# Layer 1 of a ternary feed-forward kernel by Strassen's seven products, on one Trainium2 core

## The chip, the core and the metric

The kernel runs on one NeuronCore of a Trainium2 chip. The core has a matrix engine (TensorE, PE in the profile; its weight loads are shown apart as PEld), a vector engine (DVE), a scalar engine (ACT), a general engine (GpSimd, POOL) and a queue that only starts transfers (SP). Each works through its own instructions in order, and semaphores tell one engine that another has finished. PE reads SBUF, the on-chip memory of 128 partitions, and writes PSUM, a small accumulation memory of eight banks of 2 KB per partition; ACT and DVE read both, POOL only SBUF. The metric is the time of one execution on the device in microseconds, lower is better; the median of the runs is given, and the profile is of one execution.

## The reference

```python
# x (128, 64, 512), conditions (128,), weights (200, 64, 64),
# W1 (2048, 512), b1 (2048,), W2 (512, 2048), b2 (512,)
w = weights[conditions]
c = jnp.einsum('bct,bcd->bdt', x, w)               # mixing by a condition

def ternary_linear(x, W, b, threshold=0.05):
    Wq = ternarize(W, threshold)                   # alpha * sign(W) * (|W| > 0.05 max|W|)
    return jnp.einsum('bsd,hd->bsh', x, Wq) + b

h = gelu(ternary_linear(c, W1, b1))                # (128, 64, 2048)
y = ternary_linear(h, W2, b2)                      # (128, 64, 512)
scale = jnp.max(jnp.abs(y)) / 7 + 1e-8             # over all of y
return x + jnp.clip(jnp.round(y / scale), -7, 7) * scale
```

The ternary weights without alpha are -1, 0 and 1, so they are exact in any type; alpha is applied once per layer behind the matmuls.

## The kernel before

**Tiling.** The 128 sequences of 64 tokens are 8192 tokens. A block is 512 of them (4 pairs of sequences); there are NB = 16 blocks. The 2048 hidden features are NH = 16 chunks of 128. The ternary weights lie in SBUF for good, as 1-byte numbers: `w1t` (per chunk 4 x 128 inputs by 128 features) and `w2t` (per chunk 128 features by 512 outputs).

**Precision.** Matmuls run on a 32-bit type that keeps fewer bits (float32r, shown as fp32r or f32). So each activation is split into a high part, rounded by ACT, and a low part, the rest, by DVE (`split`, lines 197 to 200), and each matmul is done for both. The weights are widened to the same type by POOL just before use (`widen1`, `widen2`, lines 415 to 430), into small rotating buffers `w1f` and `w2f`.

**One step** (n, hc), lines 713 to 748, is one chunk of one block. POOL widens the weights of the next step's layer 1 and of the previous step's layer 2. PE does `layer1`: 8 matmuls (4 input pieces, 2 parts) of 512 tokens into one bank, `ph`. ACT takes the bank with Gelu, bias and alpha into `hf` and rounds it to the high part, and DVE subtracts (`bend`, lines 446 to 449). Then PE does `layer2` for the chunk of two steps before (LAG = 2): 8 matmuls of 512 outputs into four banks, `py0` to `py3`, which add up over the 16 chunks of a block. When the last chunk is in, DVE writes y out of the four banks (`result`) and takes its maxima (`largest`).

**Conditioning** of the next block is spread over the steps of this one: SP loads x (`load_x`), POOL gathers the condition matrices (`fetch`) and places them on a block diagonal (`place`), and in four steps (hc 8 to 11) PE mixes one pair each (`mix`, 4 matmuls in source, 8 on the engine since they are done in full precision, of 128 columns, into a bank `pc`), from which ACT and DVE make the two parts of `x` (`condition`, lines 213 to 216).

**The order** on each engine is the order of the source: the wrapper `InOrder` (lines 43 to 51) passes every instruction through and keeps it. That is why the profile puts almost all of them on line 51, and why they are told apart by the names of their tiles.

**Ends.** Before this loop the weights are loaded and made ternary while block 0 runs in another order (lines 107 to 700). After it, the scale over all y is made, x is loaded again, and the result is written (lines 750 to 815).

**Buffers.** The pool `big` has 22 buffers of 8 KB per partition, `half` has 6 of 4 KB (w1f, w2f, hf and three for the parts of h), `ps_h` two banks, `ps_c` two, `ps_y` four. A buffer given out again makes its first writer wait for the last reader of the one before.

Of the kernel before, what the change touches and what calls it, by code (L numbers as in the profile page):

```python
# [22 lines left out]
F32 = mybir.dt.float32  # L26
# [28 lines left out]
def tile_cond_ternary_ffn(  # L55
# [26 lines left out]
    GH = NH // NG  # L82
    WCH = GH * T
    LAG = 2

    const = ctx.enter_context(tc.tile_pool(name="const", bufs=1))
    big = ctx.enter_context(tc.tile_pool(name="big", bufs=22))
    gather = ctx.enter_context(tc.tile_pool(name="gather", bufs=PAIRS))
    half = ctx.enter_context(tc.tile_pool(name="half", bufs=6))
    ps_c = ctx.enter_context(tc.tile_pool(name="ps_c", bufs=2, space=PSUM))  # L90
    ps_h = ctx.enter_context(tc.tile_pool(name="ps_h", bufs=2, space=PSUM))
    ps_y = ctx.enter_context(tc.tile_pool(name="ps_y", bufs=1, space=PSUM))
# [4 lines left out]
    def pair_of_pairs(h):  # L97
        return slice(h * PAIRS // 2, (h + 1) * PAIRS // 2)

    def load_x(n):  # L100
        xt = big.tile([P, PAIRS, T], F32, tag="big", name=f"xt_{n}")
        for h in range(2):
            js = pair_of_pairs(h)
            sp.dma_start(out=xt[:, js, :], in_=x_blk[n][:, js, :])
        return xt

# [85 lines left out]
    def parts(n):  # L194
        return [big.tile([P, NT, BLK], F32R, tag="big", name=f"x{k}_{n}") for k in range(2)]

    def split(src, hi, lo, engine=dve):

        act.copy(hi, src)
        engine.tensor_tensor(lo, src, hi, ALU.subtract)  # L200

    def mix(xt, j, pc):

        for c in range(NT):
            pe.matmul(
                out=pc[:, c, :],
                lhsT=xt[:, j, c * P : (c + 1) * P],
                rhs=diag[:, j, :],
                start=True,
                stop=True,  # L210
            )
# [179 lines left out]
    pb = ps_c.tile([P, NH], F32, tag="pc", name="pb")  # L391
    pe.transpose(pb, b1n, ident_f[:NH, :NH])
    b1t = const.tile([P, NH], F32)
    w1f0 = big.tile([P, 4, NT, P], F32R, tag="big", name="w1f0")
    turned(act, w1f0[:, 0], 0)
    hi0(2)
    hi0(3)
    turned(act)
# [5 lines left out]


    hidden = {}
    wide1 = {(0, 0): w1f0[:, 0]}
    wide2 = {}
    ypsum = {}
    ys = []  # L410
# [3 lines left out]

    def widen1(n, hc):

        w = w1f0[:, hc % 4] if n == 0 else w1f[:, hc % 2]
        pool.tensor_copy(w, w1t[:, hc])
        wide1[n, hc] = w

    def widen2(n, hc):
        if n == 0 and hc < NH - LAG:
            w = w2f0[0][:, hc % 4]
        elif n == NB - 1 and hc == NH - 1:

            w = w1f[:, 0].rearrange("p c h -> p (c h)")
        else:
            w = w2f[:, hc % 2]
        pool.tensor_copy(w, w2t[:, hc])
        wide2[n, hc] = w  # L430

# [14 lines left out]

    def bend(n, hc, ph, two, hf, engine=dve):
        act.activation(hf, ph, AF.Gelu, bias=b1t[:, hc : hc + 1], scale=alpha[1])
        split(hf, *two, engine)
        hidden[n, hc] = two  # L450

    def layer2(n, hc, js=range(PAIRS)):
        two = hidden[n, hc]
        w = wide2[n, hc]
        if hc == 0:
            ypsum[n] = [
                ps_y.tile([P, T], F32, tag=f"py{j}", name=f"py{j}_{n}") for j in range(PAIRS)
            ]
        for j in js:
            for k in range(2):  # L460
                pe.matmul(
                    out=ypsum[n][j],
                    lhsT=two[k][:, j * P : (j + 1) * P],
                    rhs=w,
                    start=(hc == 0 and k == 0),
                    stop=(hc == NH - 1 and k == 1),
                )
# [13 lines left out]

    waiting = {}
    pairs0 = {}
    ring = big.tile([P, 4, BLK], F32, tag="big", name="ring")

    def early(hc):

# [8 lines left out]
    def early_bend(hc):  # L496
        if hc % 2 == 0:
            pairs0[hc // 2] = big.tile([P, 2, 2, BLK], F32R, tag="big", name=f"h_{hc}")
        h = pairs0[hc // 2]
        bend(  # L500
            0,
            hc,
            waiting.pop(hc),
            [h[:, hc % 2, k, :] for k in range(2)],
            ring[:, hc % 4, :],
            pool if hc % 2 == 0 and hc < 10 else dve,
        )

# [111 lines left out]
    early_bend(0)  # L620
    x_next = load_x(1)
    two_next = parts(1)
    find = thresholds("w2", top_2, above.bitcast(F32)[:, :P])
    made = {}
    w2f0 = []
    puts = {}

    def put(key):
# [13 lines left out]
    def behind(hc):  # L642
        if hc in (6, 8, 10, 11):
            put({8: 7}.get(hc, hc))
        if hc in (5, 6, 8):
            largest2({5: 1, 6: 2, 8: 3}[hc])
        if hc == 7:
            signed1(3)
        if hc == 10:
            next(find)  # L650
            delta.extend(next(find))
            made[0] = signed2(0)
            next(made[0])
        if hc == 11:
            next(made[0])
        if hc == 14:
            put("2a")
        if hc == 15:
            w2f0.append(big.tile([P, 4, T], F32R, tag="big", name="w2f0"))
            widen2(0, 0)  # L660

    for hc in range(5, NH):
# [30 lines left out]
        if 8 <= hc < 8 + NG:  # L693
            sum2(hc - 8)
    cond[1] = two_next
    w1f = half.tile([P, 2, NT, P], F32R, tag="half", name="w1f")
    w2f = half.tile([P, 2, T], F32R, tag="half", name="w2f")
    hf = half.tile([P, 2, BLK], F32, tag="half", name="hf")
    widen1(1, 0)
    widen2(0, NH - LAG)  # L700


    steps = [(n, hc) for n in range(NB) for hc in range(NH)]
# [6 lines left out]
            j = hc // (NH // PAIRS)  # L710
            sp.dma_start(out=dying[t][:, j, :], in_=x_blk[3 + t][:, j, :])

    for s in range(NH, len(steps)):
        n, hc = steps[s]
        if s + 1 < len(steps):
            widen1(*steps[s + 1])
            lend(0, *steps[s + 1])
        widen2(*steps[s + 1 - LAG])
        lend(1, *steps[s + 1 - LAG])
        if n + 1 < NB:  # L720
            if hc == 0:
                x_next = load_x(n + 1)
                two_next = parts(n + 1)
                fetched = []
            if 2 <= hc < 2 + PAIRS:
                fetched.append(fetch(n + 1, hc - 2))
            if 7 <= hc < 7 + PAIRS:
                place(hc - 7, fetched[hc - 7])
        if n == NB - 1 and hc < 3:
            again.append(load_x(hc))  # L730
        ph = ps_h.tile([P, BLK], F32, tag="ph", name=f"ph_{n}_{hc}")
        layer1(n, hc, ph)
        two = half.tile([P, 2, BLK], F32R, tag="half", name=f"h_{n}_{hc}")
        bend(n, hc, ph, [two[:, k, :] for k in range(2)], hf[:, hc % 2, :])
        if n + 1 < NB and 8 <= hc < 8 + PAIRS:
            condition(n + 1, hc - 8, x_next, two_next)
            cond[n + 1] = two_next
        if hc == LAG:
            for j in range(PAIRS):
                largest(n - 1, j)  # L740
        if s == len(steps) - 1:
            break
        if s == NH + 1:
            alpha_2()
        layer2(*steps[s - LAG])
        if steps[s - LAG][1] == NH - 1:
            for j in range(PAIRS):
                result(n - 1, j)

    n = NB - 1  # L750
    widen2(n, NH - 1)
    lend(1, n, NH - 1)
    again += [t for t in dying]
    for _ in range(2):
        again.append(load_x(len(again)))
    dve.tensor_reduce(
# [22 lines left out]
    dve.reciprocal(inverse, scale)  # L779


    halves = []
    for i in range(6):
        m, h = len(again) + i // 2, i % 2
        xt = half.tile([P, PAIRS // 2, T], F32, tag="half", name=f"xt_{m}_{h}")
        sp.dma_start(out=xt, in_=x_blk[m][:, pair_of_pairs(h), :])
        halves.append(xt)
    xs = [[xt[:, pair_of_pairs(h), :] for h in range(2)] for xt in again]
    xs += [halves[i : i + 2] for i in (0, 2, 4)]
    quant = flat(diag).bitcast(I8).rearrange("p (k t) -> p k t", k=PAIRS)  # L790
    AHEAD = len(xs)
    for n in range(NB):

        while len(xs) < min(AHEAD + 3 * n // 2, NB):
            xt = load_x(len(xs))
            xs.append([xt[:, pair_of_pairs(h), :] for h in range(2)])
        for h in range(2):


            q = quant[:, h * PAIRS // 2 : (h + 1) * PAIRS // 2, :]  # L800
            if n < NB - 1:
                y = res = ys[n][:, pair_of_pairs(h), :]
                act.activation(flat(q), flat(y), AF.Identity, scale=inverse)
                dve.scalar_tensor_tensor(
                    flat(y), flat(q), scale, flat(xs[n][h]), ALU.mult, ALU.add
                )
            else:
                res = xs[n][h]
                for k in range(PAIRS // 2):
                    y = ypsum[n][h * PAIRS // 2 + k]  # L810
                    act.activation(q[:, k, :], y, AF.Identity, scale=inverse)
                    dve.scalar_tensor_tensor(
                        res[:, k, :], q[:, k, :], scale, res[:, k, :], ALU.mult, ALU.add
                    )
            pool.dma_start(out=out_blk[n][:, pair_of_pairs(h), :], in_=res)
# [34 lines left out]
```

## Time and profile before

| | us |
|---|---|
| median of 3 runs | 1102.17 (1100.96 to 1102.38) |
| the profiled execution | 1102.12 |
| its span, from the first to the last instruction | 1100.4 |
| one block in the middle (238.1 to 300.0, from one block's first layer 2 to the next's) | 61.9 |
| PE busy | 1023.9 |
| ACT, POOL, DVE busy | 471.6, 466.7, 399.2 |

How to read the lines of the profile: engine, operation, the tile that is written, an arrow, the tiles that are read, then partitions x elements and types of output and input. In a group "x2040 | 514.3, 394 | 0.0" is the number of instructions, their busy time in us, the mean duration of one in ns, and the engine's idle time just before them with the operation that ended it. In the timeline a line has its start, its length and how many neighbouring instructions of one kind are merged in it; "[2.93 <-ACT h L51]" is idle time before it and what ended it. Matmuls overlap in the array, so the duration of one is longer than the time from one to the next. The chain of waits goes back from the last instruction through whatever released each; its shares say which engine set the end.

### The profile page before, as it was taken

Reading aid. Unit: us, or ns where it says so; the run is one execution under the profiler, and the core shown is the slowest. Engines: PE = TensorE matmul, PEld = TensorE weight load, DVE = VectorE, ACT = ScalarE, POOL = GpSimd, SP = SyncE. Lnnn points to the kernel's source line nnn. Section 1 sums busy time; section 2 is a strip of 40 time slices with the busy share of each in tenths; the row PEclk is TensorE's granted clock in tenths of the full one; section 3 lists DMA queues with packets and bytes.
Section 4 is the critical chain, followed back from the end, with each engine's and each line's share of the span. In section 5 each row is a group of like instructions: output and inputs, shape, how many; then the busy total and the mean of one; then the engine's idle time right before and its main releaser. Section 6 shows DMA issues by size and latency. Waiting matters only on the chain.

```text
span 1100.4 us, 13296 instructions
## 1 busy us (share of the span) xinstructions
PE 1023.9 (93%) x4830; PEld 841.4 (76%) x4832; DVE 399.2 (36%) x549; ACT 471.6 (43%) x650; POOL 466.7 (42%) x754
## 2 busy tenths in 40 slices
PE   8989999999999999999999999999999999999500
PEld 4678788888888888888888888888888888888400
DVE  6875423232322323232322423232322423232592
ACT  6965333434344433434344343434344343434491
POOL 5644535343443535343443535343443535333242
PEclk9999999999999999999999999999999999999855
DMA  9214001000101001000001001000001001111699
GB/s 327 78 39 153 5 1 44 1 5 4 38 5 38 6 1 44 1 4 6 36 4 39 6 2 43 1 4 7 35 5 39 6 3 42 39 58 39 254 416 380
DMA packets 28752, 62.01 MB, mean 56 GB/s; under 512 B 2816, under 2 KB 2960, under 8 KB 28688
## 3 DMA queue, kind: packets, MB, share of 16 engines
q1 hardware_dynamic: 22032, 42.28, 11.2%
q0 software_dynamic: 6656, 18.88, 4.4%
q8 instruction: 39, 0.64, 0.3%
q14 instruction: 25, 0.20, 0.1%
HBM read 44.38 MB, written 16.78 MB: 56 GB/s over the span
## 4 chain that ended last, share of the span: by engine, by line
PE 89%; DVE 4%; DMA 4%; ACT 2%; issue 1%; POOL 0%; POOLq 0%; DVEq 0%; ACTq 0%
PE py L51 42%; PE ph L51 40%; PE pc L51 5%; DMA out<-y 4%; PE idle L51 2%; DVE tern L51 1%; DVE top L51 1%; DVE y L51 0%; PE pt L51 0%; DVE h L51 0%; ACT diag L51 0%; ACT h L51 0%; DVE ymax L51 0%; DVE py L51 0%; ACT ring L51 0%
## 5 line engine op out<-in xcount | busy, mean ns | idle before, releaser
L51 PE MATMUL py<-w2f,h 128*128 128x512 f32 x2040 | 514.3, 394 | 0.0
L51 PE MATMUL ph<-x,w1f 128*128 128x512 f32 (+1 forms) x2056 | 507.5, 389 | 1.0 <-POOL w1f L51 0.7
L51 PEld LDWEIGHTS ph<-x,w1f 128*128 128x128 f32 x2056 | 384.5, 188 | 81.5 <-POOL w1f L51 1.0
L51 PEld LDWEIGHTS py<-w2f,h 128*128 128x128 f32 x2040 | 377.6, 189 | 80.5 <-DVE y L51 5.5
L51 ACT ACTIVATE hf<-ph,b1t,alpha_w 128x512 f32<-128x512 f32 x240 | 187.2, 780 | 554.1 <-PE ph L51 554.1
L51 DVE TENSOR_TENSOR h<-hf,h 128x512 fp32r<-128x512 f32 x240 | 166.2, 692 | 650.6 <-ACT h L51 650.6
L51 POOL CAST w2f<-w2t 128x512 fp32r<-128x512 fp8e4 x255 | 178.6, 701 | 360.1 <-PE py L51 336.3
L51 POOL CAST w1f<-w1t 128x512 fp32r<-128x512 fp8e4 x255 | 163.6, 643 | 192.8 <-PE ph L51 180.2
L51 ACT CAST h<-hf 128x512 fp32r<-128x512 f32 x240 | 148.8, 620 | 7.6
L51 PEld LDWEIGHTS pc<-diag,xt 128*128 128x128 f32 x512 | 66.6, 192 | 4.6
L51 POOL DMA_INDIRECT wg<-in_L_cond_weights,rows x64 | 63.6, 994 | 13.7 <-issue 6.6
L51 PE MATMUL pc<-diag,xt 128*128 128x128 f32 x512 | 67.6, 276 | 0.0
L51 DVE TENSOR_TENSOR x<-pc,x 128x512 fp32r<-128x512 f32 x64 | 43.6, 684 | 10.2 <-ACT x L51 10.2
L51 DVE SCALAR_TENSOR_TENSOR y<-py,alpha_w,b2b 128x512 f32<-128x512 f32 x60 | 40.8, 742 | 0.1
L51 ACT ACTIVATE diag<-y,inverse 128x1024 int8<-128x1024 f32 x30 | 34.3, 1148 | 12.1 <-DVE inverse L51 8.8
L51 ACT CAST x<-pc 128x512 fp32r<-128x512 f32 x64 | 37.1, 582 | 5.5 <-PE pc L51 5.5
L51 POOL DMA_DIRECT2D out<-y x30 | 21.8, 728 | 40.0 <-DVE y L51 25.9
L51 DVE TENSOR_REDUCE ymax<-y 128x1 f32<-128x512 f32 x60 | 36.9, 676 | 0.0
L51 DVE SCALAR_TENSOR_TENSOR y<-diag,scale,xt 128x1024 f32<-128x1024 int8 x26 | 32.4, 1282 | 6.4 <-DMA xt<-in_x 4.9
L51 POOL COPY diag<-wg 64x64 f32<-64x64 f32 x128 | 29.6, 231 | 8.3 <-DMA wg<-in_L_cond_weights,rows 4.5
L51 PE MATMUL idle<-junk,ones_b 128*128 128x512 bf16 x63 | 16.7, 433 | 3.4 <-POOL junk L51 3.3
L51 PEld LDWEIGHTS <-ones_b 128*128 128x128 bf16 x80 | 8.3, 106 | 14.9 <-issue 6.3
(91 smaller groups left out, 205.1 us busy)
## 6 DMA issues: line engine op xcount, KB each, us to landing
xt<-in_x SPq DMA_DIRECT2D x60, 512.0 KB, 4.7
out<-y POOLq DMA_DIRECT2D x30, 512.0 KB, 12.8
nat<-in_L_ffn_W SPq DMA_DIRECT2D x7, 1024.0 KB, 13.2
nat<-in_L_ffn_W SPq DMA_DIRECT2D x2, 512.0 KB, 12.8
wg<-in_L_cond_weights,rows POOLq DMA_INDIRECT x64, 2.4
w1t<-in_x SPq DMA_DIRECT2D x4, 256.0 KB, 2.7
w2t<-in_x SPq DMA_DIRECT2D x4, 256.0 KB, 2.6
out<-xt POOLq DMA_DIRECT2D x2, 512.0 KB, 9.5
```

Of the source, the lines that this page charges most:

```text
L51: return lambda *args, **kw: self._tc.keep_in_program_order(make(*args, **kw))
```

## The change

For blocks 2 to 11 (`SEVEN`), two chunks of layer 1 are computed together. The product of a 2 x 2 scheme of halves (halves of the 512 inputs; chunk 2k and chunk 2k+1 of features; the first and the second 64 tokens of each pair of sequences, `b11`, `b12`, `b21`, `b22`) is formed from seven products of halves in the order of Winograd's variant, in place of eight.

- Weights: four combinations `w1s` of w1t (`combine`), made by DVE once, in block 1. `widen7` widens, per pair of chunks, the seven left factors in four groups. The buffers `w1f` and `w2f` now have four slots each for the whole run and are used in twos outside `SEVEN`.
- Activations: `condition7` makes, besides the halves b11, b21 and b22, four combinations `t` in full precision (DVE) and their two parts.
- `seven`: 28 matmuls of 256 tokens into three banks: `x` and `y` (the two of ps_h, which change places from pair to pair) and `z` (one of ps_c, with p4 and p5 in its halves). Some products add onto a bank that ACT has copied out before. ACT copies x, z and x into `ring` (ha and hb, the sums of the two chunks); DVE adds y, p5 and the last x; then Gelu runs in place. The layer 2 of the two chunks before is done in eight pieces (`second`, 2 matmuls each) between the products. The second chunk's Gelu is issued at the start of the next pair (`finish`), and the low parts of h by `low`.
- Loads, gathers, placing, the conditioning of the next block and the maxima of y are issued at fixed places of the pairs (`behind`); the conditioning in pairs 3 to 6.
- Buffers: big 20, half 10. Block 15's x and some reloads of x go to pairs of half buffers. Blocks 0, 1 and 12 to 15 keep the old step, now called `eight`.

```diff
-    big = ctx.enter_context(tc.tile_pool(name="big", bufs=22))
+    big = ctx.enter_context(tc.tile_pool(name="big", bufs=20))
-    half = ctx.enter_context(tc.tile_pool(name="half", bufs=6))
+    half = ctx.enter_context(tc.tile_pool(name="half", bufs=10))
...
     def bend(n, hc, ph, two, hf, engine=dve):
         act.activation(hf, ph, AF.Gelu, bias=b1t[:, hc : hc + 1], scale=alpha[1])
-        split(hf, *two, engine)
+        if engine is None:
+            act.copy(two[0], hf)
+            open_low[n, hc] = lambda: dve.tensor_tensor(two[1], hf, two[0], ALU.subtract)
+        else:
+            split(hf, *two, engine)
...
+    def combine():
+        w1s = big.tile([P, NH // 2, 4, 2 * P], F8, tag="big", name="w1s")
+        extra["w1s"] = w1s
+        s1, s2, s4, s3 = (w1s[:, :, i, :] for i in range(4))
+        for out, in0, in1, op in (
+            (s1, a21, a22, ALU.add),
+            (s2, s1, a11, ALU.subtract),
+            (s4, a12, s2, ALU.subtract),
+            (s3, a11, a21, ALU.subtract),
+        ):
+            dve.tensor_tensor(out, in0, in1, op, saturate=False)
+            yield
+
+    def groups(k):
+        w1s = extra["w1s"]
+        return (
+            ((0, 0, T, w1t_f[:, 2 * k]),),
+            ((1, 0, T // 2, w1s[:, k, 0]), (1, T // 2, T, w1t_f[:, 2 * k + 1, T // 2 :])),
+            ((2, 0, T, flat(w1s[:, k, 1:3])),),
+            ((3, 0, T // 2, w1s[:, k, 3]),),
+        )
+
+    def widen7(k, g):
+        for i, lo, hi, src in groups(k)[g]:
+            pool.tensor_copy(flat(w1f[i])[:, lo:hi], src)
...
+    def condition7(n, j, xt, two):
+        xb, xts, xl = two
+        cols = slice(j * C, (j + 1) * C)
+        pc = ps_c.tile([P, NT, P], F32, tag="pc", name=f"pc_{n}_{j}")
+        mix(xt, j, pc)
+        act.copy(xb[:, 0, :, cols], pc[:, :, :C])
+        act.copy(xl[:, 0, :, cols], pc[:, 2:, C:])
+        t, b12 = extra["t"], extra["b12"]
+        act.copy(b12, pc[:, :2, C:])
+        dve.tensor_tensor(t[:, 0], b12, pc[:, :2, :C], ALU.subtract)
+        dve.tensor_tensor(t[:, 2], pc[:, 2:, C:], b12, ALU.subtract)
+        dve.tensor_tensor(t[:, 1], pc[:, 2:, C:], t[:, 0], ALU.subtract)
+        dve.tensor_tensor(t[:, 3], pc[:, 2:, :C], t[:, 1], ALU.subtract)
+        dve.tensor_tensor(xb[:, 1, :, cols], pc[:, :, :C], xb[:, 0, :, cols], ALU.subtract)
+        dve.tensor_tensor(xl[:, 1, :, cols], pc[:, 2:, C:], xl[:, 0, :, cols], ALU.subtract)
+        t8 = t.rearrange("p a c d -> p (a c) d")
+        hi, lo = (x.rearrange("p a c d -> p (a c) d")[:, :, cols] for x in xts)
+        act.copy(hi, t8)
+        dve.tensor_tensor(lo, t8, hi, ALU.subtract)
+
+    def product(out, w, b, first):
+        for c in range(2):
+            for k in range(2):
+                pe.matmul(out=out, lhsT=w[:, c, :], rhs=b[k][:, c, :],
+                    start=(first and c == 0 and k == 0), stop=(c == 1 and k == 1),
+                    skip_group_check=True)
+
+    def seven(n, k, behind, second):
...
+        behind(0)
+        product(x, w1f[0][:, :2], b11, True)
+        act.copy(ha_2[:, 0], turned(x))
+        product(y, w1f[0][:, 2:], b21, True)
+        behind(1)
+        dve.tensor_tensor(ha_2[:, 0], turned(y), ha_2[:, 0], ALU.add)
+        product(p5, w1f[1][:, :2], t1, True)
+        product(p4, w1f[1][:, 2:], t4, False)
+        behind(2)
+        act.copy(hb_2, z.rearrange("p (h j d) -> p h j d", h=2, j=PAIRS))
+        second(0)
+        product(x, w1f[2][:, :2], t2, False)
+        act.copy(ha_2[:, 1], turned(x))
+        second(1)
+        second(2)
+        product(p5, w1f[2][:, 2:], b22, False)
+        dve.tensor_tensor(ha_2[:, 1], turned(p5), ha_2[:, 1], ALU.add)
+        second(3)
+        bend7(0, ha)
+        behind(3)
+        second(4)
+        product(x, w1f[3][:, :2], t3, False)
+        dve.tensor_tensor(
+            hb_2, turned(x).unsqueeze(1).to_broadcast([P, 2, PAIRS, C]), hb_2, ALU.add
+        )
+        low(n, 2 * k)
+        behind(4)
+        for i in range(5, 8):
+            second(i)
+        return lambda: bend7(1, hb)
...
+        def behind(i):
+            if i == 0:
+                finish()
+                widen2(*before[1])
+                if k == 0:
+                    x_next.append(load_x(n + 1))
+                    two_next.append(parts7(n + 1) if n + 1 in SEVEN else parts(n + 1))
+            if i == 1:
+                low(*before[1])
+                if leaves:
+                    widen1(n + 1, 0)
+                else:
+                    widen7(ahead, 0)
+            if i == 2:
+                if not leaves:
+                    widen7(ahead, 1)
+                if k in (0, 1):
+                    for j in (2 * k, 2 * k + 1):
+                        fetched.append(fetch(n + 1, j))
+                if k in (2, 3):
+                    for j in (2 * k - 4, 2 * k - 3):
+                        place(j, fetched[j - PAIRS])
+            if i == 3:
+                widen2(*steps[s])
+                if not leaves:
+                    widen7(ahead, 2)
+            if i == 4:
+                if not leaves:
+                    widen7(ahead, 3)
+                if 3 <= k < 3 + PAIRS:
+                    make = condition7 if n + 1 in SEVEN else condition
+                    make(n + 1, k - 3, x_next[-1], two_next[-1])
+                    cond[n + 1] = two_next[-1]
+                if k in (1, 2):
+                    for j in (2 * k - 2, 2 * k - 1):
+                        largest(n - 1, j)
```

## The prediction

> **What bounds the kernel now.** First the page: busy times, granted clock and the chain that ended last.
>
> ```profile
> PE 1023.9 (93%) x4830; PEld 841.4 (76%) x4832; DVE 399.2 (36%) x549; ACT 471.6 (43%) x650; POOL 466.7 (42%) x754
> ...
> PEclk9999999999999999999999999999999999999855
> ...
> PE py L51 42%; PE ph L51 40%; PE pc L51 5%; DMA out<-y 4%; PE idle L51 2%; DVE tern L51 1%; DVE top L51 1%; DVE y L51 0%; PE pt L51 0%; DVE h L51 0%; ACT diag L51 0%; ACT h L51 0%; DVE ymax L51 0%; DVE py L51 0%; ACT ring L51 0%
> ```
>
> PE is the bound: layer 2 (py), layer 1 (ph) and the mixing (pc) are 87% of the chain, at full clock until the output stage. ACT, DVE and POOL are under half busy, so work moved to them is free only as long as PE never waits for its result. Next, PE in order of time: what one matmul costs in a run.
>
> ```profile
> 25.32 1.12 PE L51 MATMUL ph<-x,w1f 128*128 128x256 f32 x8
> ```
> ```profile
> 500.60 1.98 PE L51 MATMUL ph<-x,w1f 128*128 128x512 f32 x8
> ```
> ```profile
> 506.04 1.05 PE L51 MATMUL pc<-diag,xt 128*128 128x128 f32 x8
> ```
>
> A merged line ends with the last matmul's own duration. 256 columns (chunk 0 of block 0 is computed in two halves, so the form is in this trace): mean 0.28, hence (1.12-0.28)/7 = 0.120 us from start to start. 512 columns: (1.98-0.39)/7 = 0.2266. 128 columns: 0.111. A half-width matmul costs 53% of a full one, not 50%. Third, the chain in order of time shows the one regular wait of PE, at each block's start: a layer-2 chunk of 1.99 instead of 1.81, of which the end of a merged line and the wait for DVE's y leave about 0.17 lost per block.
>
> ```profile
> 482.45 1.81 PE ph L51 x8
> 484.26 1.99 PE py L51 x8
> ```
>
> Fourth, the groups by shape, for the small operations that the change adds (mean ns is the number before the last bar):
>
> ```profile
> L51 ACT ACTIVATE hf<-ph,b1t,alpha_w 128x512 f32<-128x512 f32 x240 | 187.2, 780 | 554.1 <-PE ph L51 554.1
> L51 ACT CAST h<-hf 128x512 fp32r<-128x512 f32 x240 | 148.8, 620 | 7.6
> L51 ACT CAST x<-pc 128x512 fp32r<-128x512 f32 x64 | 37.1, 582 | 5.5 <-PE pc L51 5.5
> ...
> L51 ACT CAST w2t<-pt 128x1024 fp8e4<-128x1024 bf16 x8 | 8.1, 1010 | 13.5 <-PE pt L51 13.5
> ...
> L51 ACT ACTIVATION_READ_ACCUMULATOR tern<-tern 128x1 f32 x4 | 0.8, 195 | 0.0
> ```
> ```profile
> L51 DVE TENSOR_TENSOR h<-hf,h 128x512 fp32r<-128x512 f32 x240 | 166.2, 692 | 650.6 <-ACT h L51 650.6
> L51 DVE TENSOR_TENSOR x<-pc,x 128x512 fp32r<-128x512 f32 x64 | 43.6, 684 | 10.2 <-ACT x L51 10.2
> ...
> L51 DVE TENSOR_TENSOR first<-first 128x128 f32<-128x128 f32 x1 | 0.3, 293 | 0.0
> ```
>
> Last, single hand-overs in order of time:
>
> ```profile
> 90.24 1.05 PE L51 MATMUL pc<-diag,xt 128*128 128x128 f32 x8
> ...
> 91.33 0.59 ACT L51 CAST x<-pc 128x512 fp32r<-128x512 f32 x1 [1.77 <-PE pc L51]
> ```
> ```profile
> 507.05 0.62 ACT L51 CAST h<-hf 128x512 fp32r<-128x512 f32 x1
> 507.57 0.58 ACT L51 CAST x<-pc 128x512 fp32r<-128x512 f32 x1
> 507.70 0.69 DVE L51 TENSOR_TENSOR h<-hf,h 128x512 fp32r<-128x512 f32 x1 [2.93 <-ACT h L51]
> ```
> ```profile
> 1027.27 0.62 ACT L51 CAST h<-hf 128x512 fp32r<-128x512 f32 x1
> ...
> 1028.00 0.19 PEld L51 LDWEIGHTS py<-w1f,h 128*128 128x128 f32 x1 [1.10 <-issue]
> ```
> ```profile
> 1028.67 0.19 PEld L51 LDWEIGHTS py<-w1f,h 128*128 128x128 f32 x1 [0.48 <-DVE h L51]
> ...
> 1029.01 0.39 PE L51 MATMUL py<-w2f,h 128*128 128x512 f32 x1
> ```
>
> Read off: PE's end to ACT's start 0.04; ACT's end to DVE's start 0.03 (the same is taken for DVE to ACT, and on one engine behind its own result); two ACT operations that don't depend overlap by 0.09, on DVE by 0.08; a stalled PE loads weights 0.11 after ACT's end, and its second matmul starts 0.34 behind that load, that is 0.11 over the usual 0.23.
>
> **The change, part by part.** *Layer 1 of blocks 2 to 11.* A pair of chunks had 16 matmuls of 512 columns (16 x 0.2266 = 3.626 us); it gets seven products of 4 matmuls of 256 (28 x 0.120 = 3.360). All on the bounding engine: 0.266 a pair, 80 pairs, **-21.2 us**. Counted in columns alone it would be an eighth, 36 us; the fixed 13 ns of each of 12 more matmuls takes the rest. [...]
>
> *The block's start.* In the first pair of a block DVE's four y operations (742 ns each) run while PE does layer 2 of the old block; the new block's first layer 2 comes only after four products of the next pair (1.92 us). The wait goes: 10 x 0.17 = **-1.7 us**. If DVE were late, 0.17 a block comes back.
>
> *Recombining (every pair).* ACT copies x, z and x out of PSUM, DVE adds y, p5 and x. With 0.84 ns an element (from the 1024 and 512 rows out of PSUM) a 256-element ACT copy is 0.37, a 128-element one 0.26; DVE from 684 at 1.04 ns gives 0.42 and 0.28 (the 128x128 row has 0.29); Gelu now reads SBUF, 0.78 + 0.04 = 0.82 (copies differ by that: 620 against 582). In a pair without conditioning, from its first product: the copy of x that the third group's product (x += ..., at 2.37) waits for ends at 1.4; the copy of z that the b22 product (3.77) waits for ends at 2.7, or at 3.5 in a block's second pair, where y comes first; the low halves for layer 2 are over 1.5 us early. So it costs nothing in these pairs. POOL has 3.8 us of casts a pair, 5.8 with two gathers of 994 ns, of 7.0: hidden too.
>
> *Conditioning of the next block, 4 pairs in each of blocks 2 to 10.* Here the order on ACT counts. Before, a conditioning was one ACT copy (582) and one DVE subtraction (684). Now it is ACT xb, xl, b12, then four DVE differences, then ACT's copy of their high parts, then DVE's two low parts and the low part of the differences. ACT's copy waits for DVE, and behind it in ACT's queue stand the previous chunk's Gelu and high part, and then the copy of the next pair's x, for which PE waits. From the end M of the mixing's last matmul:
> xb starts 0.04, xl 0.31, b12 0.48 to 0.74; DVE's first difference 0.77 to 1.06, the second overlaps it, the third (on the first) 1.17 to 1.46, the fourth (on the third) 1.49 to 1.78; ACT's high copy 1.81 to 2.43; Gelu 2.34 to 3.16; its high part 3.19 to 3.81; copy of x 3.71 to 4.08.
> PE meanwhile: six layer-2 matmuls (until M + 1.20), 16 of 256 (1.92), two of 512 (0.45): it wants x at M + 3.58, and its second matmul at 3.70. It gets it at 4.08 + 0.11 + 0.11 + 0.12 = 4.42. **Stall 0.72 us**, four a block (the pair behind each conditioning), nine blocks (block 11 conditions block 12 in the old way: copy of x at M + 2.2, no stall): 36 x 0.72 = **+25.9 us**. The loop repeats itself: ACT and DVE are free again 0.3 us before the next M. Later waits don't add: z's copy is done at M + 5.15, wanted at 5.7.
>
> Bounds of what the trace lacks. Small ACT copies: from below the one-element row, 0.195, which shortens the chain by 0.48 (stall 0.24, the sum -14); from above a line through that row and the 512 one (0.29 and 0.39), +0.10 (0.82, the sum +7). I take the slope between 512 and 1024, as the nearest rows. Gelu at 0.78 and a restart of 0.16 instead of 0.22 would make the stall 0.62 (sum -0.6). Pieces of 64 columns: the 512 copies in and out of four pieces of 128 cost the same as whole ones (582 against 585), so nothing is added.
> [...]
>
> *Once.* DVE combines the weights in block 1: four operations over 2048 elements, 2.3 us each by the row of that length (2279), one a step of 3.63 beside 0.69: hidden. Two big buffers become four half ones; start and end load the same in the same order: 0.
>
> **Sum:** -21.2 - 1.7 + 25.9 = +3.0. The profiled execution took 1102.12 (span 1100.4), the median of the runs is 1102.17, so there is nothing to correct: **1105.2 us**.
>
> **Rivals.** *The chain is shorter than PE's cover* (faster). ACT's place in its queue decides: below 0.57 us of stall (20.7 over 36) the kernel is faster by more than 0.2%; with no stall it takes 1079, with the one-element copies 1088. For it: all ACT pieces are small and unmeasured. Against: Gelu, its high part and the high copy, 2.06 us of the chain, are in the rows. *A second wait on the same loop* (slower): were DVE's low part late, ACT's copy of z would come after PE wants it, a slack of 0.5 us; 0.3 beyond a stall of 0.72 gives +14, 1116. For it: DVE has 5.4 us of work per such pair behind one queue; against: it ran at 692 beside POOL throughout. *The products don't run at 0.120*: between layer-2 matmuls and with more waits. At 0.130 the gain is gone (28 x 0.130 = 3.64) and the time 1127. Against: mixing runs at 0.111 with waits in it.
>
> **How the numbers follow.** The worked stall 0.55 (of its range 1101.5 to 1109, sums -0.6 to +7, about a quarter falls within 0.2%, 2.2 us, what a measurement can tell from no change); shorter chain 0.26; second wait 0.13; slow products 0.06. Faster 0.25, same 0.15, slower 0.60. The range leaves out no stall at all and slow products: 1091 to 1116.
>
> **What would show it.** Products x8 in about 1.1 us; the 512 group of ph down to about a third; PE waiting 36 times some 0.7 us for ACT's copy of x (ring from xy), always behind a conditioning; no wait for y; block 11 about 2.3 us shorter than before and blocks 2 to 10 within 0.6 us of their 61.9. I am wrong if PE waits at other places or in other pairs, if the wait is under 0.57, or if 256 columns take other than 0.120.

## The result and the profile after

The changed kernel takes 1107.16 us (median of 6 runs, 1106.55 to 1107.36) against 1101.66 for the kernel before on the same chip: ratio 1.0049, 95% interval 1.0036 to 1.0062, so 5.5 us slower. The profiled execution took 1107.36, its span is 1105.6, 5.2 more than before.

The page after: busy times and the chain that ended last; below it the same chain line of the kernel before.

```profile
PE 1012.3 (92%) x5790; PEld 864.8 (78%) x5792; DVE 596.3 (54%) x1033; ACT 601.2 (54%) x1010; POOL 594.5 (54%) x994
...
PE 77%; ACT 9%; DVE 6%; DMA 4%; POOL 2%; issue 1%; POOLq 0%; DVEq 0%; ACTq 0%; SPq 0%
```
```profile
PE 89%; DVE 4%; DMA 4%; ACT 2%; issue 1%; POOL 0%; POOLq 0%; DVEq 0%; ACTq 0%
```

PE has less to do (1012 instead of 1024 us busy), and yet the span is longer: the chain, which was PE's alone in these blocks, now runs through ACT and DVE for 15% of the span, against 6% before. The waits of PE, from 140 to 980 us (who waited, for whom, us in total, times, longest):

```profile
PEld xy L54 <- POOL wf L54: 31.2, 36, 0.9
PE xy L54 <- ACT ring L54: 12.1, 27, 0.5
PE xy L54 <- POOL wf L54: 4.2, 9, 0.5
PEld z L54 <- ACT ring L54: 1.0, 5, 0.4
PEld py L54 <- DVE y L54: 1.0, 3, 0.3
```

36 waits of one kind, four in each of blocks 2 to 10, and 27 + 9 = 36 at the matmul behind the load: the same waits, seen twice. The wait for y at the block's start is gone (before, in the same stretch: 13 times; now 3, in the blocks that keep the old step). The view names POOL for the load. One of the 36 in order of time shows who is late:

```profile
451.95 0.61 PE L54 MATMUL pc<-diag,xt 128*128 128x128 f32 x4
...
452.32 1.64 PE L54 MATMUL py<-wf,h 128*128 128x512 f32 x6
...
452.60 0.38 ACT L54 CAST xb<-pc 128x256 fp32r<-128x256 f32 x1 [0.30 <-PE pc L54]
452.87 0.27 ACT L54 CAST xl<-pc 128x128 fp32r<-128x128 f32 x1
453.03 0.28 ACT L54 COPY mixed<-pc 128x128 f32<-128x128 f32 x1
453.34 0.29 DVE L54 TENSOR_TENSOR mixed<-mixed,pc 128x128 f32<-128x128 f32 x1 [0.32 <-ACT mixed L54]
453.55 0.81 DVE L54 TENSOR_TENSOR mixed<-pc,mixed 128x128 f32<-128x128 f32 x3
...
453.79 1.12 PE L54 MATMUL xy<-xb,wf 128*128 128x256 f32 x8
...
454.39 0.62 ACT L54 CAST xt<-mixed 128x512 fp32r<-128x512 f32 x1 [1.08 <-DVE mixed L54]
...
454.91 0.81 ACT L54 ACTIVATE ring<-ring,b1t,alpha_w 128x512 f32<-128x512 f32 x1
...
455.71 0.64 PE L54 MATMUL py<-wf,h 128*128 128x512 f32 x2
455.76 0.62 ACT L54 CAST h<-ring 128x512 fp32r<-128x512 f32 x1
...
456.28 0.37 ACT L54 COPY ring<-xy 128x256 f32<-128x256 f32 x1
...
456.76 0.54 PEld L54 LDWEIGHTS xy<-xt,wf 128*128 128x128 f32 x4 [0.86 <-POOL wf L54]
456.79 0.59 PE L54 MATMUL xy<-xt,wf 128*128 128x256 f32 x3 [0.45 <-ACT ring L54]
```

Mixing ends at M = 452.56. ACT copies three pieces, waits 1.08 us for DVE's differences, makes their high parts (454.39), then Gelu and high part of the previous chunk, and only then the copy of x, which ends at 456.65, M + 4.09. PE loads the weights 0.11 later. It had run out of work at some M + 3.6.

The new groups (mean ns is the number before the last bar):

```profile
L54 ACT ACTIVATE ring<-ring,b1t,alpha_w 128x512 f32<-128x512 f32 x160 | 130.5, 816 | 120.4 <-DVE ring L54 116.7
L54 ACT COPY ring<-xy 128x256 f32<-128x256 f32 x160 | 59.4, 371 | 6.6 <-PE xy L54 6.3
...
L54 ACT COPY mixed<-pc 128x128 f32<-128x128 f32 x40 | 11.3, 283 | 0.0
L54 ACT CAST xl<-pc 128x128 fp32r<-128x128 f32 x40 | 10.9, 272 | 0.0
```
```profile
L54 DVE TENSOR_TENSOR xt<-mixed,xt 128x512 fp32r<-128x512 f32 x40 | 31.2, 780 | 6.4 <-ACT xt L54 6.4
L54 DVE TENSOR_TENSOR mixed<-pc,mixed 128x128 f32<-128x128 f32 x120 | 30.9, 284 | 1.4
```

From the start of one pair's first product to the next pair's, the trace has 7.01 to 7.03 us for a pair without conditioning, 7.90 for the first conditioning pair, 8.64 for those behind one, 7.75 for the plain pair behind the last. So each wait costs 8.64 - 7.91 = 0.73 us. A block takes 62.64 (before 61.85); block 11, which conditions block 12 in the old way, has no such wait, its conditioning pairs take 7.91, and it takes 59.71 as a whole.

### The profile page after: what moved, and what is told of

Same layout as the page of the kernel before. It is cut to its first block, busy times and chain, and to the rows that moved or that the text cites. A ratio compares the mean times of both kernels' runs of the same rounds, so it can differ in the third digit from the quotient of the medians.

```text
span 1105.6 us, 16561 instructions
## 1 busy us (share of the span) xinstructions
PE 1012.3 (92%) x5790; PEld 864.8 (78%) x5792; DVE 596.3 (54%) x1033; ACT 601.2 (54%) x1010; POOL 594.5 (54%) x994
## 4 chain that ended last, share of the span: by engine, by line
PE 77%; ACT 9%; DVE 6%; DMA 4%; POOL 2%; issue 1%; POOLq 0%; DVEq 0%; ACTq 0%; SPq 0%
PE py L54 37%; PE ph L54 14%; PE xy L54 12%; PE z L54 7%; PE pc L54 5%; ACT ring L54 3%; DMA xt<-in_x 3%; DVE mixed L54 2%; ACT h L54 2%; ACT xt L54 2%; PE idle L54 1%; POOL wf L54 1%; DMA out<-y 1%; ACT xb L54 1%; DVE tern L54 1%
## 5 line engine op out<-in xcount | busy, mean ns | idle before, releaser
L54 PE MATMUL py<-wf,h 128*128 128x512 f32 x2048 | 545.7, 396 | 0.9 <-ACT h L54 0.7
L54 PEld LDWEIGHTS py<-wf,h 128*128 128x128 f32 x2048 | 360.7, 189 | 60.8 <-DVE y L54 2.3
L54 POOL CAST wf<-w2t 128x512 fp32r<-128x512 fp8e4 x256 | 169.1, 662 | 332.5 <-PE py L54 308.5
L54 DVE TENSOR_TENSOR h<-ring,h 128x512 fp32r<-128x512 f32 x251 | 187.3, 747 | 233.5 <-ACT h L54 233.5
L54 POOL CAST wf<-w1t 128x256 fp32r<-128x256 fp8e4 (+1 forms) x255 | 186.8, 734 | 93.7 <-PE ph L54 58.0
L54 ACT ACTIVATE ring<-ring,b1t,alpha_w 128x512 f32<-128x512 f32 x160 | 130.5, 816 | 120.4 <-DVE ring L54 116.7
L54 PE MATMUL ph<-x,wf 128*128 128x512 f32 (+1 forms) x776 | 191.3, 389 | 1.0 <-POOL wf L54 0.7
L54 PEld LDWEIGHTS ph<-x,wf 128*128 128x128 f32 x776 | 144.0, 188 | 31.9 <-POOL wf L54 1.5
L54 ACT CAST h<-ring 128x512 fp32r<-128x512 f32 x256 | 158.9, 621 | 8.2
L54 POOL CAST wf<-w1s 128x256 fp32r<-128x256 fp8e4 (+1 forms) x240 | 125.0, 539 | 0.2 <-PE ph L54 0.2
```

Source lines behind the costliest of these rows:

```text
L54: return lambda *args, **kw: self._tc.keep_in_program_order(make(*args, **kw))
```

## The experiments

All stand on the changed kernel and were timed beside the kernel before on the same chip. Two theories stood against the first one: that POOL's cast is late, as the view of waits names it, and that DVE is late by the mass of its work.

**The high part late.** ACT's copy out of mixed, and DVE's low part of it, go behind the next pair's copy of z.

```diff
-        act.copy(hi, t8)
-        dve.tensor_tensor(lo, t8, hi, ALU.subtract)
+        open_high.append(high)          # the two lines above
...
         act.copy(hb_2, z.rearrange("p (h j d) -> p h j d", h=2, j=PAIRS))
+        high_now()
```

> Nothing is left out; ACT's copy of the high parts of the four differences (xt from mixed) and DVE's low part of them are issued in the next pair, behind ACT's copy of z. Theory (PE waits for the copy of x, which stands on ACT behind a copy that waits for DVE): from the end M of the mixing, Gelu at 0.66, its high part until 2.1, the copy of x until 2.4, wanted at 3.58: none of the 36 waits of 0.73 us is left, so 26 us less than the changed kernel: 1081 (1078 to 1086), about 20 under the kernel before. Rival, POOL's cast of the third weight group is late, as the profile names it (36 waits of PEld for wf): POOL's order is the same, so 1107. Rival, DVE is late with the additions: its work is the same and only moved by 2 us, so some 1095 to 1107.

1080.33 us, ratio 0.9815 (0.9798 to 0.9831). ACT in order of time in a conditioning pair of this kernel:

```profile
439.84 0.28 ACT L54 COPY mixed<-pc 128x128 f32<-128x128 f32 x1
440.00 0.84 ACT L54 ACTIVATE ring<-ring,b1t,alpha_w 128x512 f32<-128x512 f32 x1
...
440.87 0.62 ACT L54 CAST h<-ring 128x512 fp32r<-128x512 f32 x1
...
441.40 0.37 ACT L54 COPY ring<-xy 128x256 f32<-128x256 f32 x1
...
442.71 0.59 ACT L54 COPY ring<-z 128x512 f32<-128x512 f32 x1 [0.95 <-PE z L54]
...
443.20 0.62 ACT L54 CAST xt<-mixed 128x512 fp32r<-128x512 f32 x1
```

No idle time of ACT stands between b12 and the copy of x any more; it ends at 441.77, 2.39 behind the mixing's end (439.38), as worked out. All conditioning pairs take 7.91, a block 59.69. Its page's chain is PE's again:

```profile
PE 89%; DVE 4%; ACT 2%; DMA 2%; SPq 1%; issue 1%; POOL 0%; POOLq 0%; DVEq 0%; ACTq 0%
```

POOL's instructions and their order were not touched, which speaks against POOL; the run without its cast, below, settles it. DVE has the same operations, one of them later, so the mass of its work is not the cause either.

**The cost of the queue, more and less.** One ACT copy of 128 elements more ahead of b12; and, apart, two of the four differences less.

```diff
+        act.copy(extra["more"], pc[:, :2, C:])
         act.copy(b12, pc[:, :2, C:])
```
```diff
-        dve.tensor_tensor(t[:, 1], pc[:, 2:, C:], t[:, 0], ALU.subtract)
-        dve.tensor_tensor(t[:, 3], pc[:, 2:, :C], t[:, 1], ALU.subtract)
```

> One more ACT copy of 128 elements out of the mixed bank, ahead of b12, in each conditioning (its result isn't used). Theory: everything on ACT and DVE behind it comes 0.19 us later (start to start of such a copy), and PE's 36 waits grow by as much: +6.8 us on the changed kernel, 1114. Rival POOL: unchanged, 1107. Rival DVE late by its own work: ACT has 30 per cent of its time free, so 1107 to 1109.

> Leaves out the second and the fourth of DVE's four differences in the order of need (t2 and t4 of the activations; they stay zero), so that ACT's copy out of mixed waits for one step of the chain in place of three. Theory: the chain is 0.52 us shorter, the waits fall from 0.73 to 0.21, 36 x 0.52 = 19 us less: 1088 (1085 to 1092). Rival POOL: 1107. Rival DVE as a matter of its total work: 0.57 us less per pair, the same direction, 1090 to 1107, but with the wait still for DVE and not for ACT's copy of x.

1114.04 us (1.0120, 1.0103 to 1.0137) and 1088.37 (0.9882, 0.9863 to 0.9901). The pairs behind a conditioning take 8.81 and 8.10 in place of 8.64: waits of 0.90 and 0.20. A chain 0.19 longer made each wait 0.17 longer, one 0.52 shorter made it 0.54 shorter: the wait follows the chain's length nearly one to one, which mass of work on DVE wouldn't give.

**POOL's cast left out.**

```diff
                 widen2(*steps[s])
-                if not leaves:
-                    widen7(ahead, 2)
```

> Leaves out POOL's cast of the third weight group in the pairs of blocks 2 to 11, so that these products use the weights of an earlier pair; POOL has 0.6 us less work a pair and nobody waits for that group. Theory (the wait is ACT's, the name of POOL only that of the other semaphore): the 36 waits stay at 0.73 us, 1106 to 1108. Rival, POOL late: the waits go, 1081.

1104.06 us in one run, a little below the range expected, but the 36 waits stay, now named ACT's, at 0.66 us (8.57 to 8.58 a pair). The hand-over shows where the rest went:

```profile
454.94 0.37 ACT L54 COPY ring<-xy 128x256 f32<-128x256 f32 x1
```
```profile
455.35 0.53 PEld L54 LDWEIGHTS xy<-xt,wf 128*128 128x128 f32 x4 [0.81 <-ACT ring L54]
```

The load starts some 0.05 behind the copy's end (455.31; 0.04 by the rounded lines) in place of 0.11. With POOL's cast gone the load has one semaphore to wait for and not two. The traces bear this out: in the changed kernel each of the 36 loads has a semaphore instruction of its own just ahead of it and starts 0.113 behind the copy's end; here none has one, and all 36 start at 0.050 to 0.051. The loads that wait for the copy of z, in this and the other kernels, have none either and start at 0.050 to 0.052. So in these traces the loads with a second semaphore to wait for started 0.06 us later. The waits of this run are 0.07 shorter, and 36 x 0.07 = 2.5 us are most of the 3.1 us less.

**The Gelu first.** Another way out of the same queue: the second chunk's Gelu and high part ahead of the copy out of mixed.

```diff
+        hook()                 # Gelu and high part of the second chunk
         act.copy(hi, t8)
```

> Nothing is left out; the second chunk's Gelu and high part are issued ahead of ACT's copy of the high parts of the differences instead of behind it. Theory: b12 until 0.74 behind M, Gelu 0.66 to 1.47, its high part 1.50 to 2.12, the copy out of mixed 2.03 to 2.65, the copy of x 2.56 to 2.93, wanted at 3.58: no wait for x; the low part of the second chunk comes behind the low part of the differences, so z's copy ends at 4.8 and is wanted at 5.0: 1081 to 1085. Rival POOL: 1107. Rival DVE: the second chunk's low part is no earlier than before (behind the differences' low part), so 1107.

1090.93 us (0.9906, 0.9887 to 0.9924), 6 us above what was expected. The waits for x are gone, but 36 others stand in their place, for the copy of z; the pairs take 8.23, so each is 0.32 us (0.24 behind the first conditioning of a block, 8.15). The view of waits, DVE and POOL of this kernel:

```profile
PEld z L54 <- ACT ring L54: 16.1, 38, 0.5
```
```profile
455.66 0.98 DVE L54 TENSOR_TENSOR xt<-mixed,xt 128x512 fp32r<-128x512 f32 x1 [0.34 <-ACT xt L54]
456.56 0.88 DVE L54 TENSOR_TENSOR h<-ring,h 128x512 fp32r<-128x512 f32 x1
```
```profile
455.48 0.62 POOL L54 CAST wf<-w1t 128x512 fp32r<-128x512 fp8e4 x1 [0.35 <-PE xy L54]
456.04 0.85 POOL L54 CAST wf<-w1s 128x256 fp32r<-128x256 fp8e4 x1
456.85 0.85 POOL L54 CAST wf<-w1t 128x256 fp32r<-128x256 fp8e4 x1
```

The copy of z waits for the second chunk's low part, which stands on DVE behind the low part of the differences, and both took 0.9 to 1.0 us in place of 0.69, beside POOL casts that themselves took 0.85 in place of 0.40. Two runs take these apart: the two casts moved to later in the pair; and the two low parts exchanged on DVE.

```diff
-                    widen7(ahead, 1)      # at i == 2
...
                     widen7(ahead, 2)      # at i == 3
+                    widen7(ahead, 1)
```
```diff
-        dve.tensor_tensor(lo, t8, hi, ALU.subtract)
+        open_diff.append(lambda: dve.tensor_tensor(lo, t8, hi, ALU.subtract))
...
+            if i == 2:
+                diff_now()        # issues it, behind low(*before[1])
```

> Nothing is left out; the kernel with the Gelu first (e2), and POOL's two casts of the second weight group issued behind those of the third instead of early in the pair. In e2 PE waits 0.32 us for the copy of z in 36 pairs; there two of DVE's subtractions took 0.88 and 0.96 us in place of 0.69, both beside these casts. Theory (DVE's subtractions of two SBUF tensors are held up by POOL's back-to-back casts): they take 0.69 again, z is copied 0.45 us earlier and the wait goes: 1081 (1079 to 1084). Rival, the queue alone makes z late: 1091, as e2.

> Nothing is left out; the kernel with the Gelu first (e2), and DVE's low part of the differences issued in the next pair, behind the low part of the second chunk and the addition of y, in place of ahead of them. POOL's order is that of e2. Theory (z's copy waits for the low part of the second chunk, which stood on DVE behind the low part of the differences): the low part of the second chunk comes 1.1 us earlier even if the casts stretch it to 0.9, so z is in time: no wait, 1080 (1079 to 1082). Rival, the casts alone make the second chunk's low part late, wherever it stands: some 1086 to 1091.

The casts later: 1083.78 us (0.9849, 0.9832 to 0.9865), the wait 0.12 in place of 0.32. The second chunk's low part is back at 0.68, but the low part of the differences still takes 0.90 to 0.98: it is held by the first group's cast, which begins before it and was not moved. So one of the two was cured, and the wait shrank by 0.20, the 0.20 that this one gave back.

The low parts exchanged: 1083.01 us (0.9834, 0.9818 to 0.9851); all 36 waits are gone, the pairs take 7.91. What is left over the expected 1080 is one wait of 0.2 us, again for z, in the second pair of blocks 3 to 11, where y comes first on DVE (9 x 0.2 = 1.8), the place for which the prediction had the least slack. It too goes with a cast: there the second chunk's low part begins 0.05 us behind a cast and takes 0.89, where in the changed kernel it begins 0.03 to 0.04 behind the same cast and takes 0.68, and PE doesn't wait.

So the wait for z needs both, the place in DVE's queue and the casts. The exchange takes the low part of the differences (0.98) out of the way, z is copied 1.2 us earlier, and the wait is gone; the second chunk's low part isn't held there either (0.68), but 0.20 more would not bring the wait back. The two delays by casts add 0.29 + 0.19 = 0.48, more than the wait of 0.32, so without them there should be none in the old order either; this is worked out from the rows, as no run took both away.

**The consumer moved.** On the changed kernel, the product that waits for x goes behind three pieces of layer 2.

```diff
         second(0)
-        product(x, w1f[2][:, :2], t2, False)
-        act.copy(ha_2[:, 1], turned(x))
         second(1)
         second(2)
+        product(x, w1f[2][:, :2], t2, False)
+        act.copy(ha_2[:, 1], turned(x))
```

> Nothing is left out; the changed kernel with the third group's product on x issued behind three pieces of layer 2 in place of one, so PE wants the copy of x 0.91 us later and nothing moves on ACT, DVE or POOL. Theory: the copy ends at 4.09 behind M and is wanted at 4.49, so the wait for x goes; but the b22 product now follows at 4.97, and the copy of z ends at 5.2: a second wait of 0.47 us (with the loading of the weights) takes its place, 36 x 0.47 = 17 us: 1098 (1094 to 1101). Rival, the copy of x was the only late one: 1081. Rival, the stall comes from PE's own order of narrow and wide matmuls: 1107.

> Nothing is left out; the kernel with the high part late (e1), and the third group's product issued behind three pieces of layer 2, so that PE changes between narrow and wide matmuls six times a pair in place of eight. A pair without conditioning took 7.02 us in e1, where 28 x 0.120 + 16 x 0.2266 is 6.99. If each change between the widths costs 4 ns, the pair becomes 7.01 and the time 1079.6; if the 0.03 is from elsewhere (other engines' traffic), the pair stays at 7.02 and the time at 1080.3.

1097.53 us (0.9970, 0.9958 to 0.9983): the waits for x are gone and 36 for z have taken their place, as foreseen, 8.30 a pair in most against 7.93 for this order without a wait, so 0.37 (0.54 behind the first conditioning of a block). The same move on the kernel with the high part late: 1081.89 (0.9831, 0.9815 to 0.9848), a plain pair 7.03. A plain pair of the first repair took 7.01 to 7.03. Fewer changes of width did not make PE faster here; this guess is wrong.

**The best version** is the first, the high part late: 1080.33 us, 1.85% below the kernel before (1.69 to 2.02%). Its interval overlaps those of the two runs at 0.9831 and 0.9834; that it is ahead of them rests on the traces, where a block of it takes 59.69 us and one of theirs 59.84 and 59.90.

## Why the prediction was right, and what it mis-sized

- *Direction, mechanism and place: right.* 36 waits, four a block, each behind a conditioning, none in block 11 nor behind a plain pair, for ACT's copy of x, at the end of the chain that was written out. Predicted M + 4.08, measured M + 4.09. Moving one copy on ACT, with DVE's low part that depends on it, removed them all, so this is shown.
- *The wait: 0.72 predicted, 0.73 measured.* 36 x 0.734, the mean, = 26.4 for 25.9. The slopes from the rows held: 371 for 0.37, 283 and 272 for 0.26, 284 for 0.28, Gelu 816 for 0.82. The sign hung on them: with the lower bound that the prediction gives for the small copies its sum was -14, and the rows before the run could not rule that out.
- *The products, -21.2, and the wait for y, -1.7: the sum was too good.* With all waits of the conditioning gone a block takes 59.69 against 61.85 before: 2.16 a block, 21.6 in ten, for 22.9. The wait for y did go. The step that was mis-sized is 28 x 0.120 + 16 x 0.2266 = 6.99 us a pair: it takes 7.02. In the plain pairs the 16 wide matmuls take 3.71 from start to start (3.63 worked out), many of them 0.23 to 0.24, and the 28 narrow ones 3.31 (3.36): 0.03 a pair, over 2 us in 80. In lines of the first repair's kernel, the two wide ones at 442.51 take 0.47 to the next start, where two at 0.2266 take 0.45:

```profile
441.56 1.12 PE L54 MATMUL z<-xt,wf 128*128 128x256 f32 x8
442.51 0.63 PE L54 MATMUL py<-wf,h 128*128 128x512 f32 x2
442.98 0.63 PE L54 MATMUL xy<-xt,wf 128*128 128x256 f32 x4
```

Why the wide ones are slower between narrow ones stays open; fewer changes of width did not help. The prediction's account of the gain has a slip: the eighth of 36 us counts the fixed 13 ns (an estimate from its rows, 2 x 0.120 - 0.2266 us) too, so 12 more of these explain 12.8 of the 15 us between 36 and 21.2, not the whole.

- *The sum.* About -21.6 + 26.4 = +4.8, and 0.4 of a single wait (0.2, in block 10) and of the start and the end: +5.2 in the span, for +3.0. Both errors went the same way, and as the two large terms nearly cancel, an error of a tenth in both, the other way, would have left nothing of the difference (2.2 + 2.6 = 4.8). One sign that the prediction named did not come: blocks 2 to 10 were to lie within 0.6 us of their 61.9 and are 0.8 above it. Block 11 is 2.1 shorter, for 2.3.
- *The rivals.* The second wait did not occur in the changed kernel, but it was next in line: two of the repairs that cured the first wait only uncovered it. The argument against it, that DVE "ran at 692 beside POOL throughout", did not carry over to the new order of casts: the low parts of h took 747 on average and those of the differences 780 in the changed kernel (the last section has the rows with a cast beside them).
- *The view of waits* names POOL for waits that were ACT's. In the timeline POOL's cast of this group (the third group's, here merged with the fourth's behind it) had ended by 452.4, before the pair's first product at 453.79; leaving it out left the waits.

```profile
451.43 0.96 POOL L54 CAST wf<-w1s 128x512 fp32r<-128x512 fp8e4 x2
```

## What to carry over

When work is moved to engines that are half idle, don't ask how much of it there is but where each result stands in its engine's queue, and follow the longest chain of hand-overs to the instruction for which the bound engine waits: here ACT was 54% busy, and one copy of 0.62 us in the wrong place cost more than an eighth of a layer gave. A copy that waits for another engine should be issued behind everything that is already ready and wanted sooner. And when one wait is cured, work out the next one on the same loop before timing the cure.

## What the runs showed of the hardware

DVE's subtractions of two SBUF tensors (128x512) were not always 0.69 us, and POOL's casts not always 0.61 and 0.40. Which of the two began first decided who was held up. In the main loops of all the traces (140 to 980 us), 482 subtractions, 47 of them in the changed kernel, began 0.06 us or more behind a cast that had over 0.2 us to go. Each took 0.69 and the rest of that cast, less 0.13 to 0.16 us, up to 1.09 in all; in the lines above 0.98 with 0.44 left, and 0.88 with 0.33 left. In 115 of them, 10 in the changed kernel, no further cast followed, so one cast was enough and it need not be a row of them. A cast that began during a subtraction was held in the same way: the one of 256 elements took 0.85 to 0.88 in place of 0.40, that of 512 up to 1.09 in place of 0.61. Where the two began within 0.05 us of each other, either could be the one that was held. In the main loop of the kernel before, every overlap had the subtraction first, so the casts took up to 0.79 and the subtractions 0.69. DVE operations with one operand in PSUM kept their times (in the changed kernel 284, 425 and 691 ns for 128, 256 and 512 elements). Why the two hold each other up is not shown by these runs.
